# A four-layer graph network on one core: where the last layer's bias, stores and final test stand in the engines' queues, and which engine makes the first unit's subtractions

## The chip, the cores and the metric

The program runs on one core of a Trainium2 chip. The time is that of one execution on the device, in microseconds; the median of three executions before the change is 2066.45 us (2065.35 to 2071.23). The engines are TensorE (PE, with its weight loads PEld), VectorE (DVE), ScalarE (ACT), GpSimd (POOL) and SyncE (SP), which here issues nearly all DMAs of the last layer. Each engine works through its own queue in order, and they meet at semaphores.

## The reference, cut to what matters

The input is x (32 graphs, 512 nodes, 64 features) and one 512 x 512 adjacency. Four layers follow each other, each a residual on a normalized and rectified x. The change is in the last, a graph attention with eight heads and an output attention of the same form:

```python
def gat_layer(x, graph, W, b):
    h = x @ W
    s = jnp.einsum('bnd,bmd->bnm', h, h) * graph
    s = jnp.where(s == 0.0, NEG_INF, s)
    a = jax.nn.softmax(s, axis=2)
    return jnp.einsum('bnm,bmd->bnd', a, h) + b
heads = jax.vmap(lambda W, b: gat_layer(flow_x, graph, W, b))(Wh, bh)   # 8 heads of 128
cat = ...                                   # the heads side by side: B, N, 1024
x = jax.nn.leaky_relu(cat, negative_slope=0.01)
out = gat_layer(x, graph, W_out, b_out)     # 64 features
return jax.nn.leaky_relu(out, negative_slope=0.01)
```

```python
h = jnp.maximum(_layernorm(x, axis=-1), 0.0)
x = x + _L3_gnn_ref(h, adj, L3_gnn_Wh, L3_gnn_bh, L3_gnn_W_out, L3_gnn_b_out)
return x
```

## The kernel before

x stays in SBUF for the whole kernel. Layers 0 to 2 run first, in some 450 us. Then layer 3 runs as a sequence of 144 units. A unit is a pair of attentions over 512 nodes, side by side: 128 units of class `Heads` (two heads of one graph, L473) and 16 of class `Out` (the output attention of two graphs, L584). Heads units come first; an Out unit is put into the sequence some units after the heads that it needs, the first eight of them spread through the middle and the last eight at the end.

A unit passes through these steps. `scores` (L365): four blocks r of 128 rows, two matmuls each, into a PSUM tile of pool `ps_s`, which has two buffers. `maxima` (L375, VectorE): the mask is added, the row's extreme is kept, and the masked scores go to SBUF as `p_att`. `spread_out` and `spread_in` (L387, L396): a transpose on VectorE, four small DMAs to DRAM (`top_row`) and a broadcast DMA back (`topb`, 512 KB), all on SP. `shift` (L403, GpSimd): the broadcast maxima are subtracted, one instruction of 128 x 1024 for each block. `exps` (L409, ScalarE): the exponentials; those of the odd blocks go to PSUM, into a buffer of the same pool `ps_s`. `join` (L415, VectorE): an odd block's exponentials in PSUM plus the even block's in SBUF, written back; this frees the PSUM buffer for scores of a later unit. `totals`, `totals_out`, `recips`, `recips_out`, `recips_in` (L429 to L462): the sums of the exponentials by matmul, copied by ScalarE, moved by DMA so that the reciprocal is a small operation, and broadcast back as `recb`. `values` (L418): the matmuls with the values, into `av`. `normalize` (L469, VectorE): `av` times `recb` gives `o_att`.

A Heads unit then multiplies by its weights (`y_pe`) and adds the bias on ScalarE and VectorE (`y_act`, `y_dve`); `product` (L593) multiplies the result by W_out for the Out unit. An Out unit does `y_act` (L637), which adds b_out to `o_att` in place on ScalarE; `back` (L640), four transposes on TensorE and a scaled copy on ScalarE; `back_dve` (L650); `back_pool` (L655), which adds x on GpSimd; and `store` (L662), two DMAs of 128 KB on SP.

The order on every engine is the order of the program text: all five engines are under a manual schedule here. `period(t)` (L710) writes one period of it, and t runs from -1 to 149. In period t each step is called for another unit: `unit(lag)` is unit t - lag, so `now` is unit t, `ahead` is t + 1, shifts, exps and joins belong to unit t - 1, sums and values to t - 2, the normalization to t - 3, the product or back step to t - 4, `back_pool` and `store` to t - 5. Steps of units that don't exist do nothing.

`any_zero` (L668) is the final test. It reduces two small arrays of smallest magnitudes, on VectorE with three tiny transposes on TensorE between, to a flag. After layer 3 the program reads the flag and, if it is set, computes everything again in a general form; with these inputs it isn't. Before the change the test is called at the end of period 144, the first that has no scores and no `now` unit.

Of the kernel before, what the change touches and what calls it, by code (L numbers as in the profile page):

```python
# [10 lines left out]
OP = mybir.AluOpType  # L11
# [11 lines left out]
def fast_form(  # L23
# [25 lines left out]
    nc = tc.nc  # L49
# [266 lines left out]
    class Pair:  # L316
# [27 lines left out]
        def y_pe(self):  # L344
            pass

        def y_act(self):
            pass

# [50 lines left out]
                self.top_row.rearrange("(o r) p -> o (r p)", o=1).to_broadcast([P, 2 * N]),  # L400
            )

        def shift(self, r):  # L403
            nc.gpsimd.tensor_tensor(self.p[r], self.p[r], self.topb, OP.subtract)  # L404

# [176 lines left out]
    class Out(Pair):  # L584
# [49 lines left out]
        def less_next(self, k, j):  # L634
            return self.gD[:, j // 2, halves(k)]

        def y_act(self):  # L637
            nc.scalar.activation(self.o, self.o, AF.Identity, bias=b_out2, scale=1.0)  # L638

        def back(self):  # L640
# [27 lines left out]
    def any_zero():  # L668

        def across(src, rows, name):  # L670
            ps = ps_m.tile([P, P], F32, name=name, tag="m")
            n = src.shape[0]
            nc.tensor.transpose(ps[:rows, :n], src, ident[:n, :n])
            return ps[:rows, :n]

        own = tiny.tile([P, 1], F32, name="own")
        nc.vector.tensor_reduce(own, least, AX.X, OP.min)
        two = tiny.tile([1, 2], F32, name="two")
        nc.vector.tensor_reduce(two[:, 0:1], across(own, 1, "own_ps"), AX.X, OP.min)
        best = tiny.tile([B // 2, 2], F32, name="best")  # L680
        nc.vector.tensor_reduce(
            best,
            across(least_out, B // 2, "out_ps").rearrange("b (k f) -> b k f", k=2),
            AX.X, OP.max,
        )
        worst = tiny.tile([B // 2, 1], F32, name="worst")
        nc.vector.tensor_reduce(worst, best, AX.X, OP.min)
        nc.vector.tensor_reduce(
            two[:, 1:2], across(worst, 1, "worst_ps"), AX.X, OP.min
        )  # L690
        flag = tiny.tile([1, 1], F32, name="flag")
        nc.vector.tensor_reduce(flag, two, AX.X, OP.min)
        nc.vector.scalar_tensor_tensor(
            again, flag, 0.0, unsound, op0=OP.is_equal, op1=OP.max
        )
# [6 lines left out]
    def planned(units, products):  # L702

        class Nothing:
            def __getattr__(self, name):
                return lambda *args: None

        nothing = Nothing()

        def period(t):  # L710
            def unit(lag):
                return units[t - lag] if 0 <= t - lag < len(units) else nothing

            now, ahead = unit(0), unit(-1)
            for r in range(2, C):
                now.scores(r)
            unit(3).recips_in()
            unit(1).shift(0)
            unit(1).exps(0)
            unit(2).totals()  # L720
            unit(2).totals_out(1, nc.scalar)
            u, h = products.get(t - 1, (None, 0))
            if u and h == H - 1:
                u.keep_product()
            unit(1).shift(2)
            unit(1).exps(2)
            for r in range(2, C):
                now.maxima(r)
            now.spread_out()
            unit(2).totals_out(0, nc.sync)  # L730
            now.spread_in()
            for r in range(2):
                ahead.scores(r)
            unit(4).y_pe()
            unit(4).y_act()
            unit(3).normalize()
            for r in range(2):
                ahead.maxima(r)
            unit(4).back()
            unit(4).y_dve()  # L740
            unit(4).back_dve()
            unit(1).shift(1)
            unit(1).exps(1)
            for j in range(C):
                unit(2).values(j)
            u, h = products.get(t, (None, 0))
            if u:
                u.product(h)
            unit(2).recips()
            unit(2).recips_out()  # L750
            unit(1).join(1)
            unit(1).shift(3)
            unit(1).exps(3)
            unit(5).back_pool()
            unit(-2).make_gs()
            unit(5).store()
            unit(1).join(3)
            unit(-3).features(3)
            unit(-2).judge_product()
            unit(1).make_v()  # L760
            unit(-4).make_hx()
            unit(-2).make_g()
            for step in range(3):
                for lag, odd in ((step - 7, 0), (step - 11, 1)):
                    u = unit(lag)
                    if getattr(u, "i", None) == 0 and u.b % 2 == odd:
                        u.features(step)
            if t == len(units):
                any_zero()

        return period
# [1025 lines left out]
def gnn_stack_kernel(tc: tile.TileContext, *args: bass.AP):  # L1797
    nc = tc.nc
    with tc.tile_pool(name="flag", bufs=1) as pool:
        again = pool.tile([1, 1], mybir.dt.int32, name="again")  # L1800
        fast_form(tc, *args, again)
        with tc.If(nc.values_load(again[0:1, 0:1])):  # L1802
            general_form(tc, *args)
# [35 lines left out]
```

## Time and profile before

| | |
|---|---|
| median of three runs | 2066.45 us (2065.35 to 2071.23) |
| profiled execution, its own time | 2070.2 us |
| its span in the profile | 2068.4 us |
| mean granted TensorE clock | 0.985 |
| busy: TensorE, VectorE, GpSimd, ScalarE | 96%, 86%, 69%, 59% |
| first subtraction of layer 3, last normalization | 466.6 us, 2057.1 us |
| last subtraction ends | 2038.2 us |

A row of a timeline gives the start in us from the span's start, the length, the engine, the line of the kernel, the operation with what it writes and reads, how many instructions are merged into the row, and in brackets the engine's idle time before the first of them with what ended it. A row of waits gives who waited for whom, the total in us, how many times, and the longest. PEclk is the share of full speed that TensorE's clock had, in tenths, in each of 40 equal slices of the span.

### The profile page before, as it was taken

What the parts mean: (1) busy time and instruction counts of PE and PEld (TensorE: products, weight loads), DVE (VectorE), ACT (ScalarE), POOL (GpSimd) and SP (SyncE); (2) the same over time, 40 slices, a digit from 0 to 9 for tenths busy, and PEclk for the clock granted to TensorE, in tenths of its full rate; (3) what the DMA queues carried; (4) which work ended last, traced back from release to release, by engine and by line L of the source; (5) the groups of instructions that cost most, each with busy time, mean ns of one, the idle gap of its engine ahead of it and who ended that gap; (6) DMA issues with size and microseconds to landing.
All of it is one profiled execution on the core that took longest, in us unless ns stands there. A gap on an engine that the chain in (4) does not pass through costs nothing. (4 is left out here: it accounts for less than half of the span.)

```text
span 2068.4 us, 32906 instructions
## 1 busy us (share of the span) xinstructions
PE 1982.9 (96%) x11038; PEld 808.1 (39%) x11038; DVE 1774.3 (86%) x4257; ACT 1220.4 (59%) x1944; POOL 1432.8 (69%) x697
## 2 busy tenths in 40 slices
PE   7999999997999999999999999999999999999995
PEld 4676776762333333333333333333333333333231
DVE  6699997676998889998989898989898898888993
ACT  3444443345666666766666667666666766666553
POOL 2000000008888989898888889888888888888995
PEclk9999999989999999999999999999999999999997
DMA  5000000001222222222222222222222222222222
GB/s 141 1 1 1 1 2 1 2 11 58 78 74 79 74 78 81 76 75 82 74 79 73 83 74 79 73 80 77 69 78 73 69 78 77 75 68 79 76 81 69
DMA packets 135778, 129.32 MB, mean 63 GB/s; under 512 B 92792, under 2 KB 98080, under 8 KB 135472
## 3 DMA queue, kind: packets, MB, share of 16 engines
q1 hardware_dynamic: 116368, 126.35, 20.5%
q10 hardware_dynamic: 18720, 0.59, 0.5%
q8 instruction: 88, 1.44, 0.3%
q0 software_dynamic: 512, 0.20, 0.1%
q14 instruction: 90, 0.74, 0.1%
HBM read 119.48 MB, written 5.37 MB: 60 GB/s over the span
## 5 line engine op out<-in xcount | busy, mean ns | idle before, releaser
L404 POOL TENSOR_TENSOR p_att<-p_att,topb 128x1024 f32<-128x1024 f32 x576 | 1347.8, 2375 | 202.1 <-DMA topb<-top_row 136.7
L382 DVE CUSTOM_DVE_ANT_0 p_att<-s_ps,flow_neg 128x512 f32<-128x512 f32 x1152 | 726.2, 686 | 74.4 <-PE s_ps L370 73.0
L370 PE MATMUL s_ps<-hx,g 64*128 64x512 f32 x2048 | 518.1, 615 | 21.8 <-DVE p_att L416 19.4
L413 ACT ACTIVATE p_att<-p_att 128x1024 f32<-128x1024 f32 x288 | 304.3, 1057 | 232.6 <-POOL p_att L404 219.9
L416 DVE TENSOR_TENSOR p_att<-e_ps,p_att 128x1024 f32<-128x1024 f32 x288 | 342.4, 1200 | 55.4 <-ACT e_ps L413 54.1
L413 ACT ACTIVATE e_ps<-p_att 128x1024 f32<-128x1024 f32 x288 | 295.1, 1028 | 122.1 <-POOL p_att L404 111.2
L370 PEld LDWEIGHTS s_ps<-hx,g 64*128 64x128 f32 x2048 | 174.9, 186 | 336.7 <-DVE top L382 170.5
L422 PE MATMUL av<-p_att,hd 128*64 128x512 f32 x1024 | 270.5, 607 | 0.4 <-DVE o_att L471 0.4
L422 PE MATMUL av<-p_att,hn 128*64 128x512 f32 x1024 | 264.0, 594 | 0.0
L1053 POOL TENSOR_TENSOR x<-x,bias_b 128x512 f32<-128x512 f32 x16 | 20.3, 1274 | 280.7 <-DVE hn L826 280.7
L570 DVE SCALAR_TENSOR_TENSOR cat<-y_ps,bh,cat 128x512 f32<-128x512 f32 x256 | 179.8, 744 | 0.0
L562 ACT ACTIVATE cat<-y_ps,bh 128x512 f32<-128x512 f32 x256 | 161.5, 682 | 30.1 <-PE y_ps L552 28.9
L434 PE MATMUL tot_ps<-p_att,ones 128*32 128x512 f32 x1152 | 154.0, 607 | 0.0
L552 PE MATMUL y_ps<-o_att,wh_sb 64*128 64x512 f32 x512 | 133.0, 590 | 0.0
L597 PE MATMUL gT_ps<-cat,wo_sb 128*64 128x512 f32 x512 | 131.6, 592 | 0.0
L422 PEld LDWEIGHTS av<-p_att,hn 128*64 128x64 f32 x1024 | 73.7, 137 | 146.9 <-issue 146.9
L422 PEld LDWEIGHTS av<-p_att,hd 128*64 128x64 f32 x1024 | 62.3, 136 | 166.6 <-issue 130.1
L977 PE MATMUL acc<-v,s 64*128 64x65 f32 x2048 | 123.8, 279 | 0.7 <-DVE s L963 0.4
L977 PEld LDWEIGHTS acc<-v,s 64*128 64x128 f32 x2048 | 120.9, 194 | 5.9 <-DVE o L993 1.2
L884 PE MATMUL nt_ps<-adj_t,hn 128*128 128x512 f32 x256 | 117.0, 600 | 0.8 <-DVE hn L848 0.8
L471 DVE TENSOR_TENSOR o_att<-av,recb 128x512 f32<-128x512 f32 x144 | 95.4, 663 | 23.8 <-DMA recb<-rec_row 23.1
L546 ACT COPY g<-g_ps 128x512 f32<-128x512 f32 x128 | 69.4, 589 | 71.6 <-PE g_ps L534 71.6
(181 smaller groups left out, 1987.0 us busy)
## 6 DMA issues: line engine op xcount, KB each, us to landing
topb<-top_row SPq DMA_DIRECT2D x144, 512.0 KB
recb<-rec_row SPq DMA_DIRECT2D x288, 128.0 KB
top_row<-top_t SPq DMA_DIRECT2D x576, 1.0 KB
out_dram<-y SPq DMA_DIRECT2D x32, 128.0 KB
x<-in_x_dram SPq DMA_DIRECT2D x3, 1024.0 KB
parts<-tot ACTq DMA_DIRECT2D x144, 4.0 KB
parts<-tot SPq DMA_DIRECT2D x144, 4.0 KB
rec_row<-rec_flow SPq DMA_DIRECT2D x144, 4.0 KB
```

Of the source, the lines that this page charges most:

```text
L370: nc.tensor.matmul(ps[:, k], lhsT=g[halves(k), r * P : (r + 1) * P], rhs=x[halves(k), :], start=True, stop=True,)
L382: nc.vector.tensor_tensor_reduce(out=self.p[r][:, k], in0=ps[:, k], in1=flow_neg[:, r], scale=-1.0, scalar=BIG, op0=OP.add, op1=OP.min, ac ...
L404: nc.gpsimd.tensor_tensor(self.p[r], self.p[r], self.topb, OP.subtract)
L413: nc.scalar.activation(to, self.p[r], AF.Exp, scale=-1.0)
L416: nc.vector.tensor_tensor(self.p[r], self.joined, self.p[r - 1], OP.add)
L422: nc.tensor.matmul(self.av[halves(k), :], lhsT=self.v(k, j) if j % 2 else self.less_next(k, j), rhs=self.p[j][:, k], start=(j == 0), stop= ...
L434: nc.tensor.matmul(ps[q : q + 32, :], lhsT=ones, rhs=self.p[2 * e + 1][:, k], start=True, stop=True,)
L552: nc.tensor.matmul(ps, lhsT=wh_sb[halves(k), 2 * self.i + k, :], rhs=self.o[halves(k), :], start=True, stop=True,)
L562: nc.scalar.activation(self.cat[:, k], self.y[k], AF.Identity, bias=bh01[:, h : h + 1], scale=0.01)
L570: nc.vector.scalar_tensor_tensor(self.cat[:, k], self.y[k], bh[:, h : h + 1], self.cat[:, k], op0=OP.add, op1=OP.max,)
L597: nc.tensor.matmul(self.gps[halves(k), :], lhsT=wo_sb[:, h, :], rhs=Heads.cat.pop((self.b + k, h)), start=(h == 0), stop=(h == H - 1),)
L977: nc.tensor.matmul(self.acc[k][:, r], lhsT=self.s[b // 2][halves(k), b % 2, r * P : (r + 1) * P], rhs=self.v[halves(k), b], start=(b == 0) ...
```

## The change

Four edits, all in layer 3. First, `Out.y_act` becomes `Out.bias`, called at the head of the period, ahead of the first exponential, instead of behind `y_pe`; for Heads units it does nothing, and their own `y_act` stays. Second, `any_zero` is called one period later. Third, `store` is called for unit t - 6 directly behind `recips_in`, instead of for unit t - 5 behind `back_pool`. Fourth, `shift` is given its engine; in period 1, the one that handles unit 0, all four subtractions go to VectorE, in the order 0, 2, 1, 3 with the exps of blocks 0, 2, 1 between, behind the maxima of the unit ahead.

```diff
-        def shift(self, r):
-            nc.gpsimd.tensor_tensor(self.p[r], self.p[r], self.topb, OP.subtract)
+        def shift(self, r, engine):
+            engine.tensor_tensor(self.p[r], self.p[r], self.topb, OP.subtract)
...
-        def y_act(self):
+        def bias(self):
             nc.scalar.activation(self.o, self.o, AF.Identity, bias=b_out2, scale=1.0)
...
             unit(3).recips_in()
-            unit(1).shift(0)
-            unit(1).exps(0)
+            unit(6).store()
+            unit(4).bias()
+            if t != 1:
+                unit(1).shift(0, nc.gpsimd)
+                unit(1).exps(0)
             unit(2).totals()
             unit(2).totals_out(1, nc.scalar)
...
-            unit(1).shift(2)
-            unit(1).exps(2)
+            if t != 1:
+                unit(1).shift(2, nc.gpsimd)
+                unit(1).exps(2)
...
             for r in range(2):
                 ahead.maxima(r)
+            if t == 1:
+                for r in (0, 2, 1, 3):
+                    unit(1).shift(r, nc.vector)
+                    if r < 3:
+                        unit(1).exps(r)
             unit(4).back()
             unit(4).y_dve()
             unit(4).back_dve()
-            unit(1).shift(1)
-            unit(1).exps(1)
+            if t != 1:
+                unit(1).shift(1, nc.gpsimd)
+                unit(1).exps(1)
...
             unit(1).join(1)
-            unit(1).shift(3)
+            if t != 1:
+                unit(1).shift(3, nc.gpsimd)
             unit(1).exps(3)
             unit(5).back_pool()
             unit(-2).make_gs()
-            unit(5).store()
             unit(1).join(3)
...
-            if t == len(units):
+            if t == len(units) + 1:
                 any_zero()
```

More of the change, by code (lines that the diff above doesn't have):

```diff
@@ L345, in y_pe @@
             pass
+        def bias(self):
+            pass
         def y_act(self):
@@ L635, in less_next, with bias @@
             return self.gD[:, j // 2, halves(k)]
-        def y_act(self):
+        def bias(self):
             nc.scalar.activation(self.o, self.o, AF.Identity, bias=b_out2, scale=1.0)
```

## The prediction

> **What bounds the kernel now.** I read the page first, then TensorE's waits, then the timeline at the three places that the change touches.
>
> Page, busy time and TensorE's granted clock by slice:
>
> ```profile
> PE 1982.9 (96%) x11038; PEld 808.1 (39%) x11038; DVE 1774.3 (86%) x4257; ACT 1220.4 (59%) x1944; POOL 1432.8 (69%) x697
> PEclk9999999989999999999999999999999999999997
> ```
>
> TensorE is nearly always busy, so only its holes and the two ends of layer 3 can give time. Its waits between 490 and 2030 us (total, times, longest):
>
> ```profile
> PE back_ps L643 <- ACT o_att L638: 20.7, 12, 3.0
> PE s_ps L370 <- DVE p_att L416: 9.6, 13, 1.2
> ```
>
> Two thirds of that idle time is the last product's transposes waiting for its bias. Timeline of the first such period (start, length, engine, line, idle before):
>
> ```profile
> 662.78 9.34 POOL L404 TENSOR_TENSOR p_att<-p_att,topb 128x1024 f32<-128x1024 f32 x4 [1.48 <-DMA topb<-top_row]
> ...
> 667.51 1.06 ACT L413 ACTIVATE p_att<-p_att 128x1024 f32<-128x1024 f32 x1 [0.80 <-POOL p_att L404]
> ...
> 668.47 0.70 ACT L638 ACTIVATE o_att<-o_att,b_out 128x512 f32<-128x512 f32 x1
> ...
> 669.23 0.66 PE L643 MATMUL back_ps<-ident,o_att 128*128 128x128 f32 x4 [1.84 <-ACT o_att L638]
> ...
> 673.22 1.23 DVE L416 TENSOR_TENSOR p_att<-e_ps,p_att 128x1024 f32<-128x1024 f32 x1 [0.52 <-ACT e_ps L413]
> ...
> 675.23 0.19 PEld L370 LDWEIGHTS s_ps<-hx,g 64*128 64x128 f32 x2 [0.23 <-issue]
> ```
>
> The bias sits on ScalarE behind an exp that waits for GpSimd. But look at the last two rows: the join ends at 674.45, and the scores that take over its PSUM buffer start at 675.23. A second loop (scores, maxima, DMA, four shifts on GpSimd, exp, join, scores two units on) is only 0.78 us behind TensorE there.
>
> Start of layer 3:
>
> ```profile
> 466.62 18.54 POOL L404 TENSOR_TENSOR p_att<-p_att,topb 128x1024 f32<-128x1024 f32 x8 [24.89 <-DMA top_row<-top_t]
> ...
> 474.67 1.23 DVE L416 TENSOR_TENSOR p_att<-e_ps,p_att 128x1024 f32<-128x1024 f32 x1 [6.80 <-ACT e_ps L413]
> ...
> 475.95 2.08 PE L370 MATMUL s_ps<-hx,g 64*128 64x512 f32 x4 [9.55 <-DVE p_att L416]
> ```
>
> TensorE stands 9.55 us while GpSimd makes unit 0's subtractions. End of the kernel:
>
> ```profile
> 2038.03 2.48 DVE L416 TENSOR_TENSOR p_att<-e_ps,p_att 128x1024 f32<-128x1024 f32 x2
> ...
> 2044.08 0.28 DVE L677 TENSOR_REDUCE own<-least 128x1 f32<-128x129 f32 x1
> ...
> 2045.62 1.07 PE L434 MATMUL tot_ps<-p_att,ones 128*32 128x512 f32 x8
> ...
> 2046.75 0.59 ACT L440 COPY tot<-tot_ps 128x512 f32<-128x512 f32 x1 [3.05 <-PE tot_ps L434]
> ...
> 2050.48 0.69 DVE L651 SCALAR_TENSOR_TENSOR y<-back_ps,y 128x512 f32<-128x512 f32 x1 [3.61 <-ACT y L648]
> ...
> 2051.09 0.16 DVE L451 TENSOR_REDUCE rec_flow<-parts 128x8 f32<-128x16 f32 x1
> ...
> 2053.26 1.24 SPq L465 DMA_DIRECT2D recb<-rec_row  x2
> ...
> 2057.11 0.69 DVE L471 TENSOR_TENSOR o_att<-av,recb 128x512 f32<-128x512 f32 x1 [5.63 <-DMA recb<-rec_row]
> ```
>
> The last join ends at 2040.51, its sums run only at 2045.62, and everything to the end hangs on them.
>
> [...] The join of that size here (one operand in PSUM) took 1.22 us, so I use 1.2 for a subtraction. [...] after the 2.37 us wait at 961.97 the clock averaged 0.54 from 962.5 to 966.
>
> **Part 1, first unit on VectorE.** VectorE's last maxima end at 467.87; the broadcast maxima landed by 466.62. Four subtractions, one each 1.15 (joins issued back to back start 1.13 apart), end near 472.5. In their order 0, 2, 1, 3 the third is done at 471.3, its exp (1.03) at 472.4, so the first join starts near 472.5 instead of 474.67: 2.2 us. VectorE was idle 6.80 there, which hides the 4.6 us. Behind it: scores of unit 2, their maxima, their DMA, all relative, so the 2.2 is kept. GpSimd begins unit 1 when its maxima land, near 473, not at 475.9[...]. Bounds 1.2 (slow subtractions, 1.4 each) to 2.6. I take 2.2.
>
> **Part 2, bias.** The 0.71 us moves to the front of ScalarE's period. Its input was normalized 8 us earlier, and ScalarE is idle 0.5 to 2.5 us before the first exp in all eight mid places, so it costs at most 0.2 in one of them. It removes the eight waits 1.84, 1.72, 1.48, 2.37, 2.09, 1.04, 1.54, 1.54: 13.6 us, and 1.7 of slow clock after the 2.37. What is late next: the join. It comes from GpSimd, whose shifts there began on a DMA that came from scores before the wait, so it doesn't move. The spare reads 0.78, 0.77, 0.77, 2.48, 0.77, 1.39, 0.77, 0.77 at the eight places; 0.05 is the hand-over. A period later it is 0.27 at most places, plus up to 0.65 that VectorE's queue gives back. The gain of a place is the smallest of its wait, its first spare and its second. For the first place: 1.84, 0.78 - 0.05 = 0.73, and 0.27 - 0.05 + 0.65 = 0.87, so 0.7. The last place has 0.05 a period later and gives nothing. In order I count 0.7, 0.45, 0.7, 2.4, 0.7, 0.15, 0.5, 0: 5.6 us of 15.3. A gain once made is kept, since from there on every step of both loops starts from one that came earlier by as much. In a run without the slow-clock event the fourth place gives like the others: 4. From 1922 to 2038 GpSimd is busy 114.4 of 116 us, so the waits of the eight late Outs there are worth nothing until the tail. Bounds 0 to 15.3.
>
> **Parts 3 and 2 together, the tail.** With the bias ahead, TensorE doesn't wait 3.53 at 2035.32, so values of unit 142 are done by 2036, and the last sums need only the last join (2040.51, set by GpSimd, unmoved) and no final test. Sums at 2040.55, 1.65 at half clock, copied by 2042.9 instead of 2047.34: 4.4 us, of which the test's hops (2043.1 to 2045.62) are 2.5. Next, the reciprocals waited behind the back step (ended 2051.17), which waited for its bias behind the copy. Now bias first, transposes 2042.2 to 2043.3, copy, maximum: 2044.7. The parts land about 2 us after their issue at 2042.95 (the reciprocal row takes 1.4 to 2.4 to be readable in most periods): 2045.0. So the reciprocals start at 2045.0, not 2051.09: 6.1 us. The final test then runs behind them, 2.3 us of VectorE and TensorE hops plus the values it queues behind, until about 2049.7; the normalization it could delay waits for its DMA until 2051.0. Without that cover it would cost the overlap, up to 2. Bounds 3 to 7; I take 6.1.
>
> **Part 4, stores.** Two DMA issues, 1.28 us per Out, go behind the two reciprocal reads on SP and one period later. Before, the reads were issued 1.8 to 2.8 after the reciprocal row with a store ahead, and 1.4 to 2.4 in most periods without: at most 0.3 us, on a normalization that waited 0.1 to 0.8. TensorE waited once for it (0.41): 0. At the end the read waited 1.75 either way: 0. Behind the stores on SP now stand the four top_row issues, 5.5 us after the reciprocal row; 1.8 + 1.1 + 1.28 leaves 1.2 spare. Each output tile lives a period longer; its pool has six.
>
> **Sum.** 2.2 + 5.6 + 6.1 + 0 = 13.9 us against the profiled execution's 2070.2 (span 2068.4): 2056.3. That execution lies 3.75 over the median, 2066.45, and its slow-clock event explains some 2.5 of it, so from the median I take 2.2 + 4 + 6.1 = 12.3: about 2054.
>
> **Rivals.** A, full recovery: the join moves forward with TensorE and all 15.3 comes back. 2066.45 - 2.2 - 13.6 - 6.1 = 2044.5. For it: one place had 2.48 spare. Against: 0.77 at five of eight. 12%. B, GpSimd's loop takes everything in the middle and the tail gives only the test's 2.5: 2066.45 - 2.2 - 2.5 = 2061.7, within 0.3%. Against: the spare of 0.77 is really there, and the bias stands in the tail's chain. 8%. C, slower: the stores delay top_row on SP and in its queue, straight into the loop that has 0.05 to 0.8 spare. It decides from (12.3 + 6.2)/8 = 2.3 us in each mid place; at 2.5 the time is 2066.45 - 12.3 + 20 = 2074. For it: reciprocal rows took 2.7 to 3.9 in a tenth of the periods, which eats the 1.2 spare. Against: that is one place in ten, by 1.5. 4%.
>
> **Numbers.** My forecast has 76%. Its own spread, from the bounds of parts 1 to 3 taken two at a time, is about 2049 to 2059; the range 2046 to 2061 adds the slower part of A and the faster part of B, and leaves out some 18% (most of A, half of B, C). 0.3% is 6.2 us, about what a measurement can tell: faster (forecast, A, a little of B with none of C) 0.89, same 0.07, slower 0.04.
>
> **What would show it.** Right: no subtraction on GpSimd before 472; first join near 472.5; no wait of back_ps for o_att; score matmuls waiting for the join instead, by 0.5 to 1.2 in the periods after a bias; last sums within 0.1 of the last join; reciprocals 4 to 5 us after it. Wrong: transposes of maxima later against the joins than now (C), subtractions over 1.4 us, or the final test ahead of the last normalization.

## The result, and the profile after

The changed kernel takes 2055.05 us (median of 5 runs, 2053.51 to 2058.64) beside 2066.45 for the kernel before on the same chip: ratio 0.9942, 95% interval 0.9925 to 0.9959, so 11.4 us less. On a second chip it was 2054.93 beside 2069.84, ratio 0.9929 (0.9913 to 0.9944), 14.9 less. 2054 was forecast.

The profiled execution took 2057.15 us (span 2055.4), 13.0 less than that of the kernel before. That one pair hides something: layer 3's first score matmul ran at 457.32 us after, at 453.29 before. The 4.03 us came in the first 14 us, where the inputs are loaded; nothing of the change is there, and in the second profile of the same kernel the first score is at 453.70. So all stages below are measured from a point of layer 3.

Page of the kernel after, busy time and TensorE's granted clock in 40 slices:

```profile
PE 1977.7 (96%) x11038; PEld 805.5 (39%) x11038; DVE 1777.2 (86%) x4261; ACT 1221.0 (59%) x1944; POOL 1422.7 (69%) x693
PEclk9999999989999999999999999999999999999999
```

GpSimd has four instructions fewer and VectorE four more: the first unit's subtractions. The dip to 7 in the last slice is gone. TensorE's waits of the kernel after between 490 and 2030 us (total, times, longest):

```profile
PE s_ps L373 <- DVE p_att L419: 19.9, 26, 1.2
PE av L425 <- DVE o_att L474: 2.2, 3, 1.1
PE tot_ps L437 <- DVE p_att L419: 1.8, 2, 1.2
```

The 20.7 us of waits for the bias are gone to the last one. But the wait of the score matmuls for the join has doubled, from 9.6 to 19.9: most of what was freed is now spent one door further on. The timeline of the kernel after at the first place (start, length, engine, line, idle before it):

```profile
664.45 0.70 ACT L641 ACTIVATE o_att<-o_att,b_out 128x512 f32<-128x512 f32 x1
...
668.63 0.65 PE L646 MATMUL back_ps<-ident,o_att 128*128 128x128 f32 x4
...
673.80 1.23 DVE L419 TENSOR_TENSOR p_att<-e_ps,p_att 128x1024 f32<-128x1024 f32 x1 [1.11 <-ACT e_ps L416]
...
675.08 0.30 PEld L373 LDWEIGHTS s_ps<-hx,g 64*128 64x128 f32 x4 [1.12 <-DVE p_att L419]
...
675.37 9.36 POOL L407 TENSOR_TENSOR p_att<-p_att,topb 128x1024 f32<-128x1024 f32 x4 [2.66 <-DMA topb<-top_row]
```

The bias starts 4 us ahead of the transposes, which no longer wait. The next scores do: 1.12 us, until 0.05 us after the join's end at 675.03. And in the last row GpSimd waits 2.66 us for the next unit's broadcast maxima. Start of layer 3 in the kernel after:

```profile
471.83 4.62 DVE L407 TENSOR_TENSOR p_att<-p_att,topb 128x1024 f32<-128x1024 f32 x4
473.19 1.28 ACT L416 ACT_TABLE_LOAD   x1 [5.11 <-issue]
474.49 2.00 ACT L416 ACTIVATE p_att<-p_att 128x1024 f32<-128x1024 f32 x2
...
477.44 2.36 DVE L419 TENSOR_TENSOR p_att<-e_ps,p_att 128x1024 f32<-128x1024 f32 x2 [0.98 <-ACT e_ps L416]
...
478.71 3.65 PE L373 MATMUL s_ps<-hx,g 64*128 64x512 f32 x8 [8.28 <-DVE p_att L419]
```

Four subtractions on VectorE take 4.62 us where GpSimd took 9.3 (18.54 for eight). The new row is the second: ScalarE loads its table for exp after the first subtraction has ended, 1.28 us in which it makes no exponential while VectorE goes on subtracting. In the kernel before that load ran at 464.06, in idle time. End of the kernel after:

```profile
2033.03 1.23 DVE L419 TENSOR_TENSOR p_att<-e_ps,p_att 128x1024 f32<-128x1024 f32 x1 [1.09 <-ACT e_ps L416]
...
2034.31 1.05 PE L437 MATMUL tot_ps<-p_att,ones 128*32 128x512 f32 x4 [1.17 <-DVE p_att L419]
...
2035.41 0.59 ACT L443 COPY tot<-tot_ps 128x512 f32<-128x512 f32 x1 [1.28 <-PE tot_ps L437]
...
2038.39 0.17 DVE L454 TENSOR_REDUCE rec_flow<-parts 128x8 f32<-128x16 f32 x1 [0.48 <-DMA parts<-tot]
...
2038.71 0.23 DVE L680 TENSOR_REDUCE own<-least 128x1 f32<-128x129 f32 x1
...
2043.86 0.69 DVE L474 TENSOR_TENSOR o_att<-av,recb 128x512 f32<-128x512 f32 x1 [2.65 <-DMA recb<-rec_row]
```

The last sums start 0.05 us after the last join's end (5.11 before), the reciprocals 4.13 after it (10.58 before). The final test stands behind the reciprocals and ends at 2041.2, inside the normalization's wait for its DMA.

Where the 17.1 us went that layer 3 is shorter in the two profiles (first score to end): 1.7 up to the scores of block 3 of unit 2, 1.1 up to those of unit 18, 5.0 from there to unit 84, 2.3 to unit 134, 0.2 to the last join, 6.8 from there to the end. The 5.0 holds a stretch of half clock (granted 0.50 for 3.41 us) that the kernel before had at 962.8. One pair of profiles is a thin ground for it; the experiments give a fairer figure.

### The profile page after: what moved, and what is told of

Read it like the earlier page. It is cut to its first block, busy times and chain, and to the rows that moved or that the text cites. A ratio compares the mean times of both kernels' runs of the same rounds, so it can differ in the third digit from the quotient of the medians.

```text
span 2055.4 us, 32929 instructions
## 1 busy us (share of the span) xinstructions
PE 1977.7 (96%) x11038; PEld 805.5 (39%) x11038; DVE 1777.2 (86%) x4261; ACT 1221.0 (59%) x1944; POOL 1422.7 (69%) x693
## 4 chain that ended last, share of the span: by engine, by line
PE 68%; POOL 9%; DVE 9%; DMA 6%; issue 3%; ACT 3%; SPq 1%; POOLq 0%; ACTq 0%; DVEq 0%
PE s_ps L373 17%; PE av L425 16%; POOL p_att L407 9%; PE nt_ps L897 8%; PE acc L990 6%; PE tot_ps L437 4%; DVE p_att L385 4%; PE gT_ps L600 4%; PE y_ps L555 4%; PE g_ps L537 3%; DMA topb<-top_row 2%; DVE p_att L419 2%; ACT e_ps L416 1%; PE po L917 1%; DMA recb<-rec_row 1%
```

## The experiments

In the table, "start" is from the first score matmul of layer 3 to the scores of block 3 of unit 2, "middle" from the scores of block 3 of unit 18 to those of unit 84 (the eight Outs of the middle lie in it), "tail" from the end of the last join to the end of the span, all from one profile each, in us. Blocks are counted from 0, so block 3 is the last of a unit's four; the expectations below call it the third block. Ratios are against the kernel before on the same chip, with 95% intervals.

```
kernel                          start   middle  tail    ratio
before                          24.97   719.07  27.90
e1_bias     bias alone          24.62   713.97  22.97   0.9962 [0.9948, 0.9976]
e2_test     final test alone    25.00   716.30  24.02   0.9974 [0.9963, 0.9985]
e3_first    first unit alone    23.27   717.19  28.46   1.0000 [0.9990, 1.0009]
e4_stores   stores alone        24.93   715.05  29.25   1.0003 [0.9994, 1.0011]
after       all four            23.26   714.08  21.11   0.9942 [0.9925, 0.9959]
after_again all four            23.27   713.91  20.48   0.9929 [0.9913, 0.9944]
e5_table                        23.26   714.24  20.97   0.9930 [0.9914, 0.9946]
e6_shift1                       23.26   715.11  20.67   0.9927 [0.9911, 0.9943]
e8_table2                       22.24   712.81  20.80   0.9923 [0.9906, 0.9941]
e9_last_unit                    22.23   713.53  22.96   0.9920 [0.9902, 0.9938]
f1_loop_free                    23.26   702.55  20.94   0.9801 [0.9783, 0.9819]
f2_loop_free_late_bias          23.27   712.38  23.67   0.9915 [0.9897, 0.9932]
e10_fetch                       22.24   712.89  20.48   0.9932 [0.9916, 0.9948]
```

### One part at a time

The bias alone, on the kernel before:

```diff
-        def y_act(self):
+        def bias(self):
             nc.scalar.activation(self.o, self.o, AF.Identity, bias=b_out2, scale=1.0)
...
+            unit(4).bias()
             unit(1).shift(0)
             unit(1).exps(0)
```

> The kernel before with the bias alone moved to the head of the period. My theory: no wait of back_ps for o_att in the middle; the score matmuls wait for the join instead, and the middle (unit 19 to unit 84) gains 4 to 5.6 us, not 13.6. In the tail the back step no longer holds the reciprocals, but the final test still stands ahead of the last sums: reciprocals 2 to 3.5 us earlier against the last join. Together 6 to 9 us faster than before. Rival A (TensorE alone sets the middle): 15 us or more. Rival B (the loop through GpSimd takes all): 0 in the middle, 0 to 3 in all.

The final test alone:

```diff
-            if t == len(units):
+            if t == len(units) + 1:
                 any_zero()
```

> The kernel before with the final test alone called one period later. My theory: the last sums come 2.5 us earlier, their copy 2.5 us earlier; then the reciprocals still wait for the back step, whose bias stands behind that copy, so they come 2.5 us earlier too: 2 to 3 us faster. Rival: the test and the bias hide each other, so that either alone gives nothing: 0.

The first unit's subtractions alone (the bias and the stores where they were, the test too; in period 1 nothing is subtracted on GpSimd):

```diff
...
+            if t == 1:
+                for r in (0, 2, 1, 3):
+                    unit(1).shift(r, nc.vector)
+                    if r < 3:
+                        unit(1).exps(r)
```

> The kernel before with the first unit's subtractions alone on VectorE. The profile after shows ScalarE's table load of 1.28 us behind the wait for the first subtraction, where before it lay in idle time. My theory: the first join comes about 1.3 us earlier, not 2.2, the rest of the start's gain comes from a shorter stretch at half clock, and the whole is 2 to 3 us by unit 18 and kept to the end. Rival: the gain is lost again in the loop through GpSimd, and the end moves by less than 1.

The stores alone:

```diff
             unit(3).recips_in()
+            unit(6).store()
...
-            unit(5).store()
```

> The kernel before with the stores alone put behind the reciprocals' reads, a period later. My theory: nothing that a measurement shows, between 1 us faster and 1 us slower; normalizations wait less for recb, TensorE doesn't see it. Rival C: the stores delay the maxima's DMAs, transpose to first subtraction takes over 1 us longer in the period of a store, and the kernel is over 5 us slower.

The bias alone takes 7.9 us off (5.0 to 10.8) and the test alone 5.4 (3.1 to 7.7, where 2 to 3 had been expected): ratios and intervals times 2068.8, the median of the kernel before on that chip. The medians themselves differ by 9.2 and 6.5. In the tail they overlap: 4.9 and 3.9 us each, 6.8 together, against the tail of before. The two other kernels with that same tail, e3_first and e4_stores, have 28.46 and 29.25 there for its 27.90, so these gains may be up to 1.4 larger.

The middle is shorter where the bias was moved: 713.9 to 714.2 in the four runs after, after_again, e1_bias and e5_table (which changes nothing there), 715.1 to 719.1 in the four without it (before, e2_test, e3_first, e4_stores). Their means differ by 2.9 us, and the shortest of the old order is only 0.8 above the longest of the new: the size is rough. It is also not waits alone. Each of the four old-order profiles has one stretch of 3.41 us at half clock in the middle (granted 0.50 in the kernel before; from 962.8, 960.6 and 961.4, in e4_stores from 671.5), and none of the four with the early bias has one. Each begins within 1.2 us of the end of a wait for the bias (2.37, 2.26, 2.54 and 1.85 us). Half of 3.41 is 1.7: by this estimate up to 1.7 of the 2.9 us is slow clock that went with the old order. Such a wait alone did not bring it in a kernel below that has the waits back, up to 2.34 us (f2_loop_free_late_bias): it has no such stretch there.

The first unit gains its 1.7 us in the trace of e3_first, but its time can't be told from that of before (the interval is about 2 us to either side; the medians differ by 1.4). The stores are worth nothing: not the loss of rival C, nor a gain.

### Does the loop through the join limit the middle?

The decisive pair. The first kernel takes work out of the loop: it leaves out block 1's subtraction in every unit but the first, and block 1's exp takes block 0 in its place, so that its results are not the reference's. The second is the same with the bias in its old place.

```diff
         def exps(self, r):
...
-            nc.scalar.activation(to, self.p[r], AF.Exp, scale=-1.0)
+            source = self.p[0 if r == 1 and self is not flow[0] else r]
+            nc.scalar.activation(to, source, AF.Exp, scale=-1.0)
...
             if t != 1:
-                unit(1).shift(1, nc.gpsimd)
                 unit(1).exps(1)
```

> The changed kernel with block 1's subtraction left out in every unit but the first (its exp reads block 0 instead), so 2.37 us less of GpSimd in each period of the loop from scores to join. Between the third block's scores of unit 18 and of unit 84, TensorE waits 8.6 to 10.2 us for the join in the changed kernel, and the stretch takes 714.0. Theory (the loop that ends in the join took the bias's place): these waits fall to under 2, and the stretch to 705 to 707. Rival (TensorE's own work, or the Outs' added load, sets the pace, and the wait only shows it): the stretch stays at 712 to 714.

```diff
             unit(6).store()
-            unit(4).bias()
...
+            unit(4).bias()
             unit(4).back()
```

> The run before, with the Outs' bias back in its old place, so that the bias alone is compared with the loop free. Theory: the eight waits of the last product's transposes for the bias, 11.9 to 13.6 us in the stretch of units 18 to 84, are back, and the stretch is 10 to 13 us longer than in the run before (716 to 719): with the loop out of the way the bias is worth all of its waits. Rival (the bias is worth 3 us whatever the loop does): 2 to 4 us longer.

The largest entry of TensorE's waits in the stretch from unit 18 to unit 84: first of after_again,

```profile
PE s_ps L373 <- DVE p_att L419: 10.2, 15, 1.2
```

then of f1_loop_free,

```profile
PE av L426 <- DVE o_att L475: 1.0, 3, 0.6
```

then of f2_loop_free_late_bias:

```profile
PE back_ps L647 <- ACT o_att L642: 13.3, 8, 2.3
```

With the loop free the wait for the join is not small but absent, and the middle is 702.55, 11.4 us shorter than with the loop (I had said 7 to 9). With the bias late in that kernel, the eight old waits are back and the middle is 9.8 us longer: just under what the theory gave (10 to 13), and far from the 2 to 4 of its rival. Up to block 3 of unit 83 the two differ by 11.4 us; 1.6 of it is lost at unit 84, behind a late write of unit 82's maxima that only f1_loop_free has (3.15 us to its read, 1.07 in the other; such writes come below). So the same move of the same instruction is worth 9.8 us with the loop out of the way and 2.9 with it. In the kernel before, two things ended within a microsecond of each other, and the change removed one.

A smaller unloading did nothing there. Block 1's subtraction went to VectorE in the 13 periods that run an Out's back step and still subtract:

```diff
+            out_back = isinstance(unit(4), Out)
+            if out_back:
+                unit(1).shift(1, nc.vector)
...
-                unit(1).shift(1, nc.gpsimd)
+                if not out_back:
+                    unit(1).shift(1, nc.gpsimd)
```

> The changed kernel with block 1's subtraction on VectorE instead of GpSimd in the 16 periods that have an Out unit's back step. If GpSimd's chain of four subtractions, through the join, is what keeps TensorE from the full 13.6 us of the removed waits, the joins of those periods come about 2.3 us earlier, the waits of the scores for them after a back step vanish, and the middle (unit 18 to unit 84, 714 us in the changed kernel) falls by 5 to 8 us; the stretch from unit 134 to the last join falls by 2 to 5. Rival 1: something else holds TensorE there, and the middle stays within 1.5. Rival 2: VectorE and GpSimd hold each other up on two SBUF inputs, VectorE's subtraction takes over 2 us or GpSimd's over 2.6, and nothing is won or 2 to 5 us are lost.

The middle is 715.1, not shorter. This exchange takes 2.37 us from GpSimd but puts 1.2 to 1.4 on VectorE there, which is in the same loop, and only in every ninth period; that this is why is not tested. From unit 134 to the last join it gained 1.5 us (118.4 for 119.9). Timeline of e6_shift1 there, GpSimd and then VectorE:

```profile
2010.14 7.02 POOL L407 TENSOR_TENSOR p_att<-p_att,topb 128x1024 f32<-128x1024 f32 x3 [1.14 <-DMA topb<-top_row]
...
2015.37 2.87 DVE L407 TENSOR_TENSOR p_att<-p_att,topb 128x1024 f32<-128x1024 f32 x1
```

VectorE's subtraction took 2.87 us here, the twelve others 1.21 to 1.95. GpSimd's third ended at 2017.16, and 2017.16 + 1.08 is VectorE's end: it had stood still. At 2025.7 GpSimd lost instead, 3.38 for 2.37. In both cases the second ran only behind the first: from the end of the first it took 1.08 us on VectorE (1.22 in the first unit of the kernel after) and 2.23 on GpSimd (2.37). So these subtractions didn't overlap, and moving one could save there only what VectorE is faster by, 2.37 - 1.22 = 1.15 us.

### The table for exp

The load of 1.28 us is the one thing in the start that the prediction had not counted. A tiny exp was put ahead of it, first in period 0:

```diff
+            if t == 0:
+                nc.scalar.activation(tiny.tile([P, 1], F32, name="warm3"), eps, AF.Exp)
             for r in range(2):
                 ahead.scores(r)
```

> The changed kernel with one tiny exponential put on ScalarE in period 0, so that the table of exponentials is loaded ahead of the wait for VectorE's first subtraction. If that load of 1.28 us is what took the start from the expected 2.2 to 1.7, the first exp starts 1.2 to 1.3 us earlier against the start of layer 3, and scores of unit 2 come 1.0 to 1.3 us earlier. Rival: the first exp waits for VectorE or for the broadcast anyway, and nothing moves. The total, at most 1.3 us, is below what the runs can tell.

This told nothing: the tiny exp ran at 440.88, and a square root at 454.89 loaded its own table after it (1.28 us for that load in the kernel after, at 456.90), so exp's was loaded again at 469.89 behind the same wait. The second attempt put it behind that square root:

```diff
             unit(4).bias()
+            if t == 1:
+                nc.scalar.activation(tiny.tile([P, 1], F32, name="warm3"), eps, AF.Exp)
             if t != 1:
                 unit(1).shift(0, nc.gpsimd)
```

> The changed kernel with one tiny exp on ScalarE at the head of unit 0's second period, behind the last square root, so that the 1.28 us load of the exp table falls into idle time. If the load is what the first join still waits for: first subtraction's exp ends 16.8 us after the first score matmul of layer 3 (18.2 in the changed kernel), first join starts at 19.1 (20.1), the third block's scores of unit 2 at 22.2 (23.26), about 1.0 us in all. If something else is late next (VectorE's own four subtractions, the half clock): the load moves and the scores of unit 2 stay within 0.3 of 23.26.

Timeline of e8_table2 (its first score is at 453.62):

```profile
464.38 1.28 ACT L724 ACT_TABLE_LOAD   x1
...
469.50 2.06 ACT L416 ACTIVATE p_att<-p_att 128x1024 f32<-128x1024 f32 x2 [3.62 <-issue]
...
472.71 2.36 DVE L419 TENSOR_TENSOR p_att<-e_ps,p_att 128x1024 f32<-128x1024 f32 x2
```

The load is in idle time, and the first join starts 19.09 us after the first score (20.12 in the changed kernel, 21.38 before). The scores of block 3 of unit 2 come at 22.24 (23.26): the load had cost 1.02 us, and the whole start is worth 2.7 when it is hidden. Nothing further appears behind the load: the exp starts 0.02 us after its end in the changed kernel, where ScalarE had been idle 5.11 us ahead of it. Why the load stood ahead of the first exp's waits in one kernel and behind them in the other is not settled here.

### The last unit on VectorE too

```diff
-            if t != 1:
+            if t not in (1, len(units)):
...
+            if t == len(units):
+                for r in (0, 2, 1, 3):
+                    unit(1).shift(r, nc.vector)
+                    if r < 3:
+                        unit(1).exps(r)
             unit(3).normalize()
```

> As the run before, and the last unit's four subtractions on VectorE too, ahead of the normalization queued there (GpSimd does 9.4 us of them in the changed kernel, with VectorE half idle). If GpSimd's subtractions set the last join: the join of unit 143 ends 4 to 5 us earlier against the third block's scores of unit 134 (115 to 116 instead of 118.4 to 120.5), and the end 2 to 4.5 us earlier, since the chain of the output before it may be late next. If the Outs' own chain (reciprocals, DMA, normalization) sets the end: the join is earlier, and the end moves by under 1 us.

The last join comes 2.9 us earlier against unit 134 (117.76 for 120.63 in e8_table2), the end 0.7 us: the second theory, the Outs' own chain. The four subtractions stand ahead of an Out's normalization on VectorE, and the sums of the last unit are queued behind the values that need it, so that they start 2.16 us after the last join (0.05 in the changed kernel). In e9_last_unit's timeline:

```profile
2025.08 1.97 PE L425 MATMUL av<-p_att,gD 128*64 128x512 f32 x4 [3.87 <-DVE o_att L474]
```

Four of these matmuls take 1.08 us in the kernel after at a granted clock of 1.00, and 1.97 here, behind a wait of 3.87 us; in the kernel before they took 1.98 at a granted clock of 0.50 (2036.37), behind a wait of 3.53. But 0.50 was granted there behind one of 2.37 too (962.8).

### A late write, and an instruction fetch

Why was the 1.4 us that the first place gains given back a period later? TensorE's scores of block 3 of unit 20 come 20.64 us after those of unit 18 (22.01 before), those of unit 21 at 32.67 (32.14 before). SP's queue and the DMA queues of the kernel after at that place:

```profile
667.59 1.44 SPq L395 DMA_DIRECT2D top_row<-top_t  x4
...
671.55 0.34 SPq L401 DMA_DIRECT2D topb<-top_row  x1
```

```profile
q8 instruction: 1, 0.02, 1.4%
```

The four writes of unit 19's maxima end their issue at 669.03, and the read that waits for them is issued 2.52 us later; in the kernel before it was 0.96. In the same 4.1 us the kernel after has one transfer of 16 KB on the queue of kind "instruction" (the last row), 0.92 us long, starting 1.63 us after the first write; the same stretch of e2_test, with the old order, has none. The run has 88 of them, one for each 251 of TensorE's 22076 matmuls and weight loads, so I take them for TensorE's fetches: by that reading TensorE, ahead by 1.4 us, needed its next instructions earlier, and the fetch met the writes. The 14 profiles hold 48 such reads that were issued over 2.4 us after the last write; 47 have a fetch that starts 1.47 to 2.31 us after the first write, the other one at 2.64. (204 other fetches in that window came with no delay so long, so it takes more than the moment.) The 48 are not independent: 44 stand at the same four places, units 19, 82, 102 and 122, in profile after profile. Unit 19's and unit 82's are among them in all eight profiles with the early bias and TensorE's instructions as in the change, and in none of the five with the bias late. To test it, TensorE was given 28 more instructions ahead of layer 3, on top of e8_table2:

```diff
         ps = acc("own_ps", [1, P])
-        nc.tensor.transpose(ps, own, ident)
+        for _ in range(15):
+            nc.tensor.transpose(ps, own, ident)
```

> The run with the early table load, and 14 repeats of one tiny transpose on TensorE at 351 us, in layer 1 or 2, so that TensorE's instruction count runs 28 ahead in all of layer 3. If the 16 KB transfers of the queue of kind instruction[...] are what makes the writes of the maxima's row land late in the periods of units 19 and 82 (2.69 and 2.70 us from the last write to the read's issue, 0.94 to 1.03 in the kernels with the old order): they now fall about 3 us earlier, beside those writes, and the two read 0.9 to 1.2; so do units 102 and 122 (2.5 to 3 in all kernels). The gain of the first place is kept: from the third block's scores of unit 18 to those of unit 21 it takes 31.2 us instead of 32.56; the stretch of units 18 to 90 is 1.5 to 3 us shorter than 778.6. Rival (the new order of ScalarE's or SP's queue delays them): 19 and 82 stay at 2.5 to 2.8, and the stretch within 1 us of 778.6. The 14 transposes cost under 1.5 us ahead of layer 3.

Half of it came. Unit 19's read was issued 0.93 us after the last write and unit 102's 1.01 (2.56 in e8_table2), the scores of block 3 of unit 21 came at 31.06, as the theory had it, and the cycle of nine periods took 96.29 us instead of 97.79. But unit 82 stayed at 2.69 and unit 122 at 2.49, with a fetch 1.65 and 1.80 us after the first write, and new ones appeared, at units 39, 142 and 79:

```profile
1312.76 1.61 SPq L396 DMA_DIRECT2D top_row<-top_t  x4
...
1316.99 0.34 SPq L402 DMA_DIRECT2D topb<-top_row  x1
```

The stretch from unit 18 to unit 90 is 778.7 (778.6 without). So the delay went with the fetch and not with the order of ScalarE's or SP's queue, which is the same in both, and unit 19's was worth 1.5 us; but 28 instructions did not clear every meeting, and the sum of the collisions stayed. What sets the moment of a fetch remains open.

e8_table2 (0.9923) and e9_last_unit (0.9920) lie below the changed kernel (0.9942 and 0.9929), but within its interval: their 1.0 us in the start is shown by the traces alone.

## Why the prediction was right, step by step

**Start: 2.2 predicted, 1.7 measured.** Each subtraction was 1.15 apart as priced, and GpSimd's first ran at 476.73, which is 472.70 on the clock of before, as written ("near 473"). The step that failed is "its exp (1.03) at 472.4": it left out the table load, which fell behind the first exp's wait. The join gained 1.3 instead of 2.2; with the load hidden (e8_table2) it gained 2.3. The scores of block 3 gained 0.4 more than the join, which the prediction hadn't counted. In the kernel before they waited for unit 0's second join, which came 2.30 us after the first:

```profile
476.97 1.22 DVE L416 TENSOR_TENSOR p_att<-e_ps,p_att 128x1024 f32<-128x1024 f32 x1 [1.08 <-ACT e_ps L413]
...
478.25 2.08 PE L370 MATMUL s_ps<-hx,g 64*128 64x512 f32 x4 [0.23 <-DVE p_att L416]
```

After the change the two joins follow each other (2.36 us for both), and TensorE goes from block 2 to block 3 without that wait. A shorter stretch at half clock, which the expectation of e3_first named, is not the cause: it lasts 10.24 us there as in the kernel before. With the load hidden the whole gain is 2.7, just above the upper bound given.

**Bias: mechanism right, 4 predicted, 2.9 measured.** It cost ScalarE nothing: in the kernel after, at seven of the eight mid places the next exp starts 0.03 us after the subtraction that it needs, and at the other one the bias had ended 2.9 us ahead of the exp. TensorE's waits for it are gone, and the score matmuls wait for the join instead, by up to 1.2 us, as written; f1 and f2 show that this join is what caps the gain. The 4 was for "a run without the slow-clock event", but all four old-order profiles have such an event, so the prediction's 5.6 is the fairer figure beside the 2.9. The step mis-sized is the second spare, "0.27 - 0.05 + 0.65", with "A gain once made is kept". The first place took 1.4 us at once and had lost all of it a period later, when unit 19's maxima landed 1.6 us late; with that write on time in e10_fetch, 1.5 us stayed. In the means of the two groups of four profiles that gave the 2.9, the gain is 4.4 us at block 3 of unit 83 and 2.9 at unit 84, behind unit 82's late write. In e10_fetch the 1.5 us won at unit 19 were lost again by unit 84, 0.6 of them behind a new late write at unit 39, so what the middle would gain without such writes stays open. Rival A (13.6) was refuted for the reason given against it. It was not wrong in kind: with the loop free, the bias is worth 9.8.

**Tail: 6.1 predicted, 6.8 measured.** The sums waited only for the join (0.05), and the reciprocals came 4.13 us after it, inside the 4 to 5 given; that is 6.45 sooner than before. "1.65 at half clock" was wrong: TensorE's granted clock was 1.00 from 2030 to 2045 in this profile, and the sums took 1.05. The test alone gave 3.9, where the prediction's sum had 2.5 for it: in e2_test the last sums start 2.00 us after the join instead of 5.11, and the back step's transposes behind them take 0.66 (their length at a granted clock of 1.00 in the kernel after) instead of 1.11 (0.50 was granted there in the kernel before). The bias alone brought the reciprocals 4.7 us closer to the join, where 2 to 3.5 had been expected of it. The test ran under the normalization's wait, 2.65 us of which were left.

**Stores: 0 predicted, 0 measured** (1.0003). Rival C's mechanism, a late top_row in the loop, does exist, but the stores don't cause it: at units 19 and 82 e1_bias has it with the stores in their old place, and e4_stores with the stores moved has not.

**Sum.** 2.2 + 4 + 6.1 = 12.3 stood against 1.7 + 2.9 + 6.8 = 11.4; the medians differ by 11.4. That this agrees to a tenth is luck: the parts come from single profiles and rough means and leave out what other stretches gave (1.1 us ahead of unit 18 and 2.5 behind unit 84 in the first pair), the interval of the total runs from 8.5 to 15.5 us, and on the second chip the medians differ by 14.9. The forecast lies between the two chips.

## What to carry to other kernels

Before removing a wait, ask what the next loop that ends in the same queue has to spare, one and two periods later: here that capped the gain. To learn which of the two limits, unload the second and put the first back, as here (9.8 us against 2.9). Where the first use of a function on ScalarE is moved, look where its table load goes (1.02 us here). In a tail, put onto every queue first what the last output's chain needs: that gave more here than eight repaired waits in the middle.

## What the runs showed of the hardware

- Transfers of 16 KB on the queue of kind "instruction" (taken here for TensorE's instruction fetches) went with late small writes: one of them (0.9 to 1.4 us long) starting 1.5 to 2.3 us after the first of four 1 KB writes came with all but one of the 48 writes whose read was issued over 2.4 us later, where 1.0 is the median; 44 of the 48 are at four places. Moving the bias (TensorE 1.4 us ahead) made such meetings at units 19 and 82; adding 28 instructions removed those of units 19 and 102 and made others at 39, 142 and 79.
- VectorE and GpSimd, each subtracting two SBUF tiles at the same time, ran one after the other: 2.87 us for 1.22, 3.38 for 2.37 (e6_shift1, two cases).
- Half clock (granted 0.50 in the kernel before) for 3.41 us came once in the middle of each of the four profiles with the bias late and the loop whole, and in none with the bias early.
- The exp table's load (1.28 us) ran behind the first exp's wait in the kernel after, at 473.19, with 1.02 us of it exposed; at 464.06 in the kernel before and 464.38 in e8_table2 it ran in idle time.
